# A graph layer on one core: weights' product before the counts, keys' products between the gathers, rows through DRAM, routing in 16 bits

## The chip, the cores and the metric

The kernel runs on one core of one Trainium2 chip. The metric is the device time of one execution in microseconds (us), as the median of several runs. A profile of one execution gives the trace; its span runs from the first to the last instruction, so the execution's own time is a little more. The engines are PE (TensorE, matrix products and transposes), DVE (VectorE), ACT (ScalarE), POOL (GpSimd) and SP (SyncE, which issues most DMAs). Each engine works through its own list of instructions in order.

## What is computed

The input is x, 1250 tokens (nodes of a graph) of 768 numbers, and 41250 edges (src, dst). The layer is, cut to what matters:

```python
xn = layer_norm(x)
out1 = gat_conv(layer_norm(xn) * g + b, ..., H=4, C=192)     # graph attention, 4 heads
out2 = gat_conv(out1, ..., H=2, C=96)                        # graph attention, 2 heads
x = x + concat([xn, out2]) @ Wu + bu + linear_attention(xn)  # q, k = elu + 1; 12 heads
y = layer_norm(x)
gate = y @ Wg + bg; scores, idx = top_k(gate, 2)             # 8 experts
x = x + sum over the two experts: score * (gelu(y @ W1 + b1) @ W2 + b2)

# gat_conv, per head, for each edge s -> d (self loops added):
e = leaky_relu(s_src[s] + s_dst[d], 0.2)
alpha = exp(e - max over d's edges) / sum over d's edges
out[d] = sum of alpha * h[s]
```

## The kernel before

The tokens stand in 10 tiles (NT) of 125 (PT); 768 is 6 chunks (KC) of 128. All products are in float32, where PE makes two passes of each, but for the one-hot products of the counts, which are bfloat16. The code is written for a framework (Tile) that schedules each engine's list itself: the source order is a guide, and work with no dependence on what stands before it in the source can be listed earlier. Semaphores, buffers (a tile's `bufs`) and memory that one pool frees for another set what waits.

*Start, 0 to 21 us.* Edge indices, the weights W1 and W2 and small vectors are loaded from SP's queue; the edges are turned; a branch (`tc.If`, L240) for unsorted edges is not taken.

*Counts and features, 21 to 215 us.* `chunk` counts the edges of 1024 a time: DVE makes two one-hot tiles (`l_hot`, `k_hot`, L335), PE multiplies them (`ec`, L350) and DVE adds the result to the count matrix AT (L356). `features(t)` normalises one tile, PE transposes it (`turn`, L319) and the copy into `xnT` is DVE's (L321). `weights()` folds W1, W2 and the attention vectors into one matrix Wg1 (transposes of W1 L394, products with W2e L405, each W2e product waiting for the reduction L383); it is called after tile 1's features. `gathered(t)` multiplies xnT by Wg1 (L430). Then AT is turned into a mask (L461 to L466).

*Graph attention, 219 to 592 us.* `attend` handles one head. For the first layer's 4 heads: the sources' scores, less their least value, are spread as one row over all partitions (`across`: 10 transposes L504 and three ACT copies L506, into `ss_row`); ten DVE instructions (`scr`, L515) take for each target the maximum over its neighbours; from that come two columns, spread as `up_row` and `dn_row` by `across` again. Then 10 steps `st`, one for each tile of sources: ACT makes two exponentials (L533, L534), DVE takes their maximum (L535) and multiplies by the counts (L536), both 125 x 1250, and PE sums: 10 products a step in layer 1 (`ag`, L548), 3 in layer 2 (L569). Each head's result goes into h2, which the second layer's 2 heads read. `w` has 3 buffers, `v` 2, `ss_row`, `up_row` and `dn_row` one.

*Keys and values.* For each tile, four products of 6 chunks (K and V, two halves each, L607) and two of `kv` (L621), with DVE's `ky` and `ke` (L611 to L614) and sums `kvacc` (L627). They stand behind attention in the source, and the scheduler lists them into attention's gaps.

*Queries and routing, 612 to 920 us.* `graph.close()` frees attention's memory, and Wo, Wq and Wu are loaded there (L588). Per tile: the query (L751), the sum of its products (`po`, L781, `u`, L792), the store, a normalise, the gate, the two best experts, and the place of each token in its expert's list. The places come from `pp` (L830: a triangle times the selection, ones times the running sum) and go, with the gate, by one-hot products into `inv` (L854: `hot` 125 x 128 times `put` 125 x 160), from which `idx` and `gs` are read at the end.

*Experts, 948 us to the end.* Rows of the normalised tokens (`xl_d` in DRAM) are gathered by index, turned (L912), multiplied by the expert's two matrices (L926, L938), scaled by the gate and added to the output by an indirect DMA. A last part handles what does not fit the 3 fixed blocks of an expert.

Of the kernel before, what the change touches and what calls it, by code (L numbers as in the profile page):

```python
# [54 lines left out]
FIX = 3  # L55
# [14 lines left out]
def gps_block(ctx: ExitStack, tc: tile.TileContext, x, src, dst, norm_g, norm_b, W1, a_src1, a_dst1,  # L70
# [60 lines left out]
    xl_d = dram.tile([N + 128, D], F32)  # L131
# [23 lines left out]
    load_tile(0)  # L155
# [4 lines left out]
    nb_row = fl.tile([96, D], F32)  # L160
    nc.sync.dma_start(W1_sb, W1.rearrange("(c p) f -> p c f", p=128))
# [6 lines left out]
    for t, a in zip(a2, (a_src2, a_dst2)):  # L168
        nc.sync.dma_start(t.rearrange("p h c -> p (h c)"), row_bcast(a, 96))
    nc.sync.dma_start(nb_row, row_bcast(norm_b, 96))  # L170

    rows = fl.tile([KC, 128], F32)
    colv = const.tile([128, KC], F32)
    nc.sync.dma_start(rows, norm_g.rearrange("(c p) -> c p", p=128))
    rows96 = fl.tile([26, 96], F32)
    col96 = const.tile([96, 26], F32)
    nc.sync.dma_start(rows96[0:8], b1.rearrange("(c p) -> c p", p=96))
    nc.sync.dma_start(rows96[8:10], b2.rearrange("(c p) -> c p", p=96))
    for k, a in enumerate((a_src1, a_dst1)):
        nc.sync.dma_start(rows96[10 + 8 * k:18 + 8 * k], a.rearrange("h (c p) -> (h c) p", p=96))  # L180
# [145 lines left out]
    with tc.tile_pool(name="ma_p", bufs=2, space=PSUM) as ma_p:  # L326
# [31 lines left out]
        def features(t):  # L358
            if 0 < t < NT - 1:
                load_tile(t + 1)  # L360
            xt = xts.pop(t)
            xn = ln.tile([PT, D], F32, name="xn")
            mv, rs = normalise(xn, xt)

            v2 = small.tile([PT, 1], F32, name="v2")
            nc.vector.tensor_scalar(v2, mv[:, 1:2], rs, rs, op0=ALU.mult, op1=ALU.mult)
            nc.scalar.activation(v2, v2, AF.Sqrt, bias=eps[:PT])
            nc.vector.reciprocal(rs2[:, t:t + 1], v2)
            turn(xnT[:, :, t * PT:(t + 1) * PT], xn, ma_p, "tr", nc.vector.tensor_copy)

        def weights():
# [6 lines left out]
            for k in range(2):  # L378
                pr = fw.tile([96, 2, D], F32, name="W1T", bufs=2).rearrange(
# [58 lines left out]
        with tc.tile_pool(name="hot", bufs=2) as hot, \  # L438
                tc.tile_pool(name="ec_p", bufs=2, space=PSUM) as ec_p:
            for t in range(NT):  # L440
# [3 lines left out]
                if t == 1:  # L444
                    weights()
# [6 lines left out]
                if t == 4:  # L452
# [27 lines left out]
    def least(ss, H):  # L480
# [9 lines left out]
        lo = small.tile([PT, 2, H], F32, name="lo")  # L490
        nc.vector.tensor_copy(lo[:, 0], p[:, 0, :H])
        nc.vector.tensor_scalar(lo[:, 1], p[:, 0, :H], -1.0, None, op0=ALU.mult)
        return lo

    def attend(ss, sd, lo, wp, rb, gather):

        def across(cols, name, bufs, bias=0.0):

            row = rb.tile([PT, N], F32, name=name, bufs=bufs)
            for g0 in range(0, NT, 4):  # L500
                n = min(4, NT - g0)
                p = four()
                for q in range(n):
                    nc.tensor.transpose(p[:, q], cols[:, g0 + q:g0 + q + 1].to_broadcast([PT, PT]),  # L504
                                        ident[:PT, :PT])
                nc.scalar.activation(row[:, g0 * PT:(g0 + n) * PT],  # L506
                                     p[:, :n].rearrange("p a b -> p (a b)"), AF.Identity, bias=bias)
            return row


        ss_row = across(ss, "ss_row", 1, lo[:, 1:2])
        top = small.tile([PT, NT], F32, name="top")
        for t in range(NT):
            scr = wp.tile([PT, N], BF16, name="scr", bufs=1)
            nc.vector.tensor_tensor_reduce(scr, ss_row, mask[:, t], 1.0, 0.0, ALU.mult, ALU.max,  # L515
                                           top[:, t:t + 1])

        nc.vector.scalar_tensor_tensor(top, top, lo[:, 0:1], sd, op0=ALU.add, op1=ALU.add)
        nc.vector.scalar_tensor_tensor(top, top, SLOPE, top, op0=ALU.mult, op1=ALU.max)
        up = small.tile([PT, NT], F32, name="up")  # L520
        dn = small.tile([PT, NT], F32, name="dn")
        sl = small.tile([PT, NT], F32, name="sl")
        nc.vector.tensor_sub(up, sd, top)
        nc.vector.scalar_tensor_tensor(dn, sd, SLOPE, top, op0=ALU.mult, op1=ALU.subtract)
        nc.vector.tensor_scalar(sl, ss, SLOPE, None, op0=ALU.mult)
        up_row = across(up, "up_row", 1)
        dn_row = across(dn, "dn_row", 1)
        for st in range(NT):


            w = wp.tile([PT, N], F32, name="w", bufs=3)
            v = wp.tile([PT, N], F32, name="v", bufs=2)
            nc.scalar.activation(w, up_row, AF.Exp, bias=ss[:, st:st + 1])  # L533
            nc.scalar.activation(v, dn_row, AF.Exp, bias=sl[:, st:st + 1])  # L534
            nc.vector.tensor_tensor(w, v, w, op=ALU.max)  # L535
            nc.vector.scalar_tensor_tensor(w, w, 2.0, AT[:, st, :N], op0=ALU.min, op1=ALU.mult)  # L536
            gather(st, w)

    lo1 = least(s1[:, :, :, 0], H1)
    with tc.tile_pool(name="wp", bufs=3) as wp, tc.tile_pool(name="rb", bufs=1) as rb:  # L540
        with tc.tile_pool(name="ag_p1", bufs=1, space=PSUM) as ag_p:
            for hd in range(H1):
                ag = ag_p.tile([PT, NT // 2, 512], F32, name="ag")

                def gather1(st, w):
# [6 lines left out]
                attend(s1[:, :, hd, 0], s1[:, :, hd, 1], lo1[:, :, hd], wp, rb, gather1)  # L552
                v = ag[:, :, :2 * CG].rearrange("p a (b c) -> p a b c", b=2)
                rd = small.tile([PT, NT // 2, 2, 1], F32, name="rd")
                nc.vector.reciprocal(rd, v[:, :, :, C2:C2 + 1])
                for t in range(NT):
                    nc.vector.scalar_tensor_tensor(h2[:, t], v[:, t // 2, t % 2], rd[:, t // 2, t % 2],
                                                   h2[:, t], op0=ALU.mult, op1=ALU.add)
# [3 lines left out]
        lo2 = least(h2[:, :, at:at + H2], H2)  # L562
        with tc.tile_pool(name="ag_p2", bufs=1, space=PSUM) as ag_p:
            for hd in range(H2):
                ag = ag_p.tile([C2 + 1, 3, 512], F32, name="ag")

                def gather2(st, w):
# [4 lines left out]
                attend(h2[:, :, at + hd], h2[:, :, at + H2 + hd], lo2[:, :, hd], wp, rb, gather2)  # L572
                for i, (a, b) in enumerate(NCH):
                    nc.scalar.copy(o2T[:, hd, a:b], ag[:, i, :b - a])
# [22 lines left out]

    for t in range(NT):
        ky = kp.tile([PT, D], F32, name="ky", bufs=2)
        va = kp.tile([PT, KC, 129], F32, name="va")  # L600
        nc.gpsimd.memset(va[:, :, 128:], 1.0)
        for k in range(2):
            half = slice(k * 384, (k + 1) * 384)
            for w in (Wk_sb, Wv_sb):
                ps = bank()
                for c in range(KC):
                    nc.tensor.matmul(ps[:PT, :384], xnT[:, c, t * PT:(t + 1) * PT], w[:, c, half],  # L607
                                     start=c == 0, stop=c == KC - 1)
                if w is Wk_sb:
                    ke = kp.tile([PT, 384], F32, name="ke", bufs=1)  # L610
                    nc.vector.tensor_add(ky[:, half], ps[:PT, :384], bk_b[:, half])  # L611
                    nc.vector.tensor_scalar(ke, ky[:, half], 0.0, None, op0=ALU.min)
                    nc.scalar.activation(ke, ke, AF.Exp)
                    nc.vector.scalar_tensor_tensor(ky[:, half], ky[:, half], 0.0, ke, op0=ALU.max,  # L614
                                                   op1=ALU.add)
                else:
                    nc.scalar.copy(va[:, 3 * k:3 * k + 3, :128],
                                   ps[:PT, :384].rearrange("p (b c) -> p b c", b=3))
            ps = bank()
            for c in range(3):  # L620
                nc.tensor.matmul(ps[:, c * 129:(c + 1) * 129],  # L621
                                 ky[:, (3 * k + c) * 128:(3 * k + c + 1) * 128], va[:, 3 * k + c],
                                 start=c == 0, stop=c == 2, skip_group_check=True)
            acc = kvacc[:, 3 * k:3 * k + 3]
            got = ps[:, :387].rearrange("p (b c) -> p b c", b=3)
            if t:
                nc.vector.tensor_add(acc, acc, got)  # L627
            else:
                nc.vector.tensor_copy(acc, got)
# [56 lines left out]
    zero = fp.tile([128, D], F32)  # L686
    nc.gpsimd.memset(zero, 0.0)
    nc.sync.dma_start(xl_d[N:], zero)
    nc.sync.dma_start(out[N:], zero)
# [4 lines left out]
    gs = fp.tile([128, NV + 1], F32)  # L694
# [4 lines left out]
    with ExitStack() as rs:  # L699
# [7 lines left out]
        def numbers(shape, pattern, base, mult, name):  # L707
            t = rp.tile(shape, F32, name=name)
            nc.gpsimd.iota(t, pattern=pattern, base=base, channel_multiplier=mult,
                           allow_small_or_imprecise_dtypes=True)  # L710
            return t
# [304 lines left out]
```

## Time and profile before

| | |
|---|---|
| median of 5 runs | 1178.35 us (1176.38 to 1179.51) |
| profiled execution | 1179.27 us |
| its span | 1177.3 us, mean granted clock 0.971 |
| PE busy, weight loads | 1077.2 us (91%), 723.4 us (61%) |
| DVE, ACT, POOL busy | 668.8 (57%), 358.1 (30%), 76.4 us (6%) |
| moved by DMA | 79.62 MB, mean 68 GB/s |

In the page's slices, each digit is the busy share of one fortieth of the span in tenths. A group's line gives busy time, mean duration of one instruction in ns, and the idle time of the engine just ahead of it with what ended it. A timeline's line gives start, length, engine, line, operation and, in brackets, the idle time before it and its releaser. The largest groups are the first layer's gathers (L548, 137.4 us of PE), the expert products (L926 and L938, 100.6 each), and on DVE the three 125 x 1250 instructions of attention (L515, L535, L536, 86 to 87 us each).

### The profile page before, as it was taken

Reading aid. Unit: us, or ns where it says so; the run is one execution under the profiler, and the core shown is the slowest. Engines: PE = TensorE matmul, PEld = TensorE weight load, DVE = VectorE, ACT = ScalarE, POOL = GpSimd, SP = SyncE. Lnnn points to the kernel's source line nnn. Section 1 sums busy time; section 2 is a strip of 40 time slices with the busy share of each in tenths; the row PEclk is TensorE's granted clock in tenths of the full one; section 3 lists DMA queues with packets and bytes.
Section 4 is the critical chain, followed back from the end, with each engine's and each line's share of the span. In section 5 each row is a group of like instructions: output and inputs, shape, how many; then the busy total and the mean of one; then the engine's idle time right before and its main releaser. Section 6 shows DMA issues by size and latency. Waiting matters only on the chain.

```text
span 1177.3 us, 12106 instructions
## 1 busy us (share of the span) xinstructions
PE 1077.2 (91%) x4583; PEld 723.4 (61%) x4583; DVE 668.8 (57%) x1366; ACT 358.1 (30%) x527; POOL 76.4 (6%) x100
## 2 busy tenths in 40 slices
PE   2699988999999999988989999999999589999993
PEld 2586656578888778544545666666666356666652
DVE  7866676669696966696922555555555422222211
ACT  2231114373737373373712211111111011111111
POOL 1000000000000000000000000000000122322321
PEclk9999998999999999989989999999999789999997
DMA  5014000000000001000083111111123527777533
GB/s 156 27 66 148 25 16 1 1 1 1 1 1 1 1 1 53 1 0 1 1 323 99 40 40 40 40 40 40 39 65 106 189 93 188 201 211 217 122 56 55
DMA packets 33283, 79.62 MB, mean 68 GB/s; under 512 B 5259, under 2 KB 13021, under 8 KB 33209
## 3 DMA queue, kind: packets, MB, share of 16 engines
q1 hardware_dynamic: 27608, 59.02, 15.3%
q0 software_dynamic: 5600, 19.66, 8.1%
q8 instruction: 40, 0.66, 0.2%
q14 instruction: 35, 0.28, 0.1%
HBM read 60.37 MB, written 18.30 MB: 67 GB/s over the span
## 4 chain that ended last, share of the span: by engine, by line
PE 70%; DVE 20%; DMA 3%; issue 2%; ACT 2%; POOL 0%; DVEq 0%; SPq 0%; POOLq 0%; ACTq 0%
PE po L781 13%; PE ph L926 8%; PE py L938 7%; PE mm L430 7%; PE mm L607 7%; PE mm L751 7%; DVE scr L515 6%; DVE w L535 5%; DVE w L536 5%; PE ag L548 3%; PE ag L569 2%; PE u L792 2%; PE px L912 2%; PE mm L405 2%; DMA w<-in_L_gnn_Wu_dram 2%
## 5 line engine op out<-in xcount | busy, mean ns | idle before, releaser
L548 PE MATMUL ag<-kept,w 125*125 125x198 f32 x800 | 137.4, 333 | 5.1 <-DVE w L536 4.9
L548 PEld LDWEIGHTS ag<-kept,w 125*125 125x125 f32 x800 | 133.5, 188 | 9.0 <-DVE w L536 9.0
L926 PE MATMUL ph<-xsT,w 128*128 128x384 f32 (+1 forms) x324 | 100.6, 470 | 1.7 <-DVE xsT L915 1.7
L938 PE MATMUL py<-w,hT 128*128 128x384 f32 x300 | 100.6, 486 | 0.0
L430 PE MATMUL mm<-Wg,xnT 128*125 128x400 f32 x240 | 91.7, 520 | 1.0 <-DVE xnT L321 0.6
L607 PE MATMUL mm<-Wv_sb,xnT 128*125 128x384 f32 x240 | 85.7, 489 | 4.8 <-DVE kvacc L627 4.8
L535 DVE TENSOR_TENSOR w<-v,w 125x1250 f32<-125x1250 f32 x60 | 86.3, 1453 | 6.6 <-ACT w L533 5.9
L781 PE MATMUL po<-w,xnT 128*125 128x384 f32 x240 | 84.8, 496 | 2.9 <-DMA w<-in_L_gnn_Wu_dram 2.9
L515 DVE CUSTOM_DVE_ANT_0 scr<-ss_row,mask 125x1250 bf16<-125x1250 f32 x60 | 87.2, 1453 | 0.5 <-ACT ss_row L506 0.2
L536 DVE SCALAR_TENSOR_TENSOR w<-w,AT 125x1250 f32<-125x1250 f32 x60 | 86.4, 1454 | 0.4
L926 PEld LDWEIGHTS ph<-xsT,w 128*128 128x128 f32 x324 | 59.7, 193 | 41.3 <-DVE xsT L915 2.3
L607 PE MATMUL mm<-Wk_sb,xnT 128*125 128x384 f32 x240 | 84.4, 486 | 0.0
L534 ACT ACTIVATE v<-dn_row,sl 125x1250 f32<-125x1250 f32 x60 | 79.3, 1333 | 16.9 <-DVE w L535 16.4
L751 PE MATMUL mm<-w,xnT 128*125 128x384 f32 x240 | 84.2, 489 | 0.0
L915 DVE COPY xsT<-px 128x384 f32<-128x384 f32 x50 | 25.5, 552 | 100.5 <-PE px L912 100.5
L781 PE MATMUL po<-w,qT 128*125 128x384 f32 x240 | 80.8, 486 | 0.0
L938 PEld LDWEIGHTS py<-w,hT 128*128 128x128 f32 x300 | 55.3, 190 | 33.9
L941 DVE TENSOR_TENSOR ys<-py,wb 128x768 f32<-128x768 f32 x25 | 23.9, 957 | 72.5 <-PE py L938 48.8
L781 PEld LDWEIGHTS po<-w,xnT 128*125 128x125 f32 x240 | 44.2, 190 | 30.5 <-DMA w<-in_L_gnn_Wu_dram 3.1
L781 PEld LDWEIGHTS po<-w,qT 128*125 128x125 f32 x240 | 44.2, 188 | 29.4
L607 PEld LDWEIGHTS mm<-Wv_sb,xnT 128*125 128x125 f32 x240 | 42.4, 187 | 31.1 <-DVE kvacc L627 6.9
L751 PEld LDWEIGHTS mm<-w,xnT 128*125 128x125 f32 x240 | 43.6, 188 | 27.6 <-ACT qT L321 0.2
(274 smaller groups left out, 1414.5 us busy)
## 6 DMA issues: line engine op xcount, KB each, us to landing
w<-in_L_ffn_W_dram SPq DMA_DIRECT2D x18, 1152.0 KB
xt<-in_x_dram SPq DMA_DIRECT2D x20, 336.0 KB
wb<-in_L_ffn_b_dram SPq DMA_DIRECT2D x9, 384.0 KB
out_dram<-xt SPq DMA_DIRECT2D x10, 336.0 KB
xl_d<-xl SPq DMA_DIRECT2D x10, 336.0 KB
W_sb<-in_L_gnn_W_dram SPq DMA_DIRECT2D x1, 2304.0 KB
Wk_sb<-in_L_mix_Wk_dram SPq DMA_DIRECT2D x1, 2304.0 KB
Wv_sb<-in_L_mix_Wv_dram SPq DMA_DIRECT2D x1, 2304.0 KB
```

The costliest lines, as they stand in the source:

```text
L430: nc.tensor.matmul(ps[:PT, :2 * (CG + 2)], xnT[:, c, t * PT:(t + 1) * PT], Wg1[:, c, 2 * k:2 * k + 2].rearrange("p h c -> p (h c)"), start ...
L515: nc.vector.tensor_tensor_reduce(scr, ss_row, mask[:, t], 1.0, 0.0, ALU.mult, ALU.max, top[:, t:t + 1])
L534: nc.scalar.activation(v, dn_row, AF.Exp, bias=sl[:, st:st + 1])
L535: nc.vector.tensor_tensor(w, v, w, op=ALU.max)
L536: nc.vector.scalar_tensor_tensor(w, w, 2.0, AT[:, st, :N], op0=ALU.min, op1=ALU.mult)
L548: nc.tensor.matmul(ag[:, t // 2, o:o + CG], w[:, t * PT:(t + 1) * PT], gw[:, st, hd], start=st == 0 and t % 2 == 0, stop=st == NT - 1, ski ...
L607: nc.tensor.matmul(ps[:PT, :384], xnT[:, c, t * PT:(t + 1) * PT], w[:, c, half], start=c == 0, stop=c == KC - 1)
L751: nc.tensor.matmul(ps[:PT, :384], xnT[:, c, tk], Wq_sb[:, c, half], start=c == 0, stop=c == KC - 1)
L781: nc.tensor.matmul(po[k][:, :384], l, r[:, k * 384:(k + 1) * 384], start=i == 0, stop=i == len(parts) - 1)
L915: nc.vector.tensor_copy(xT[:, 3 * a:3 * a + 3, j * 128:(j + 1) * 128], px[:, a, :384].rearrange("p (b n) -> p b n", b=3))
L926: nc.tensor.matmul(ph[:, :n * 128], w[0][:, o:o + 128], xT[:, c, :n * 128], start=c == 0, stop=c == KC - 1)
L938: nc.tensor.matmul(py[:, k, :384], hT[:, f, j * 128:(j + 1) * 128], w[:, o:o + 384], start=f == 0, stop=f == FC - 1)
```

## The change

1. `weights()` is called before the counts' loop. Eight small loads go from SP's queue to ACT's; the first tile of x is loaded behind W1 and W2; Wk, Wv and bk are loaded at tile 2 instead of 4.
2. The copies of turned tiles into xnT are ACT's.
3. `attend` becomes `layer`, which handles all heads. Only the first head's rows are made by `across`; the other heads' `ss_row` and their two rows (now one tile `row`, 2 buffers) are turned to rows by one transposition (`to_rows`), written to DRAM and loaded with a broadcast. The next head's maxima are written into the first five steps of the head before it, two a step. `v` has one buffer.
4. The keys' products become a generator, `keys_and_values`, of 60 pieces; attention's steps draw one each (in layer 2 three of four), and the rest is drawn after attention.
5. In routing the one-hot tiles, the triangle, ones, the selection and its running sum are float16. `inv` holds the token's number alone. The gate is stored behind the token's row in `xl_d` (776 instead of 768 columns, two small DMAs a tile) and comes back with the gathered row; one DVE copy per gathered block takes it out.

```diff
-    xl_d = dram.tile([N + 128, D], F32)
+    row_d = [dram.tile([n * NT, PT], F32, name=f"row{i}") for i, n in enumerate((H1, H2, 2))]
+    xl_d = dram.tile([N + 128, D + NE], F32)
...
-            turn(xnT[:, :, t * PT:(t + 1) * PT], xn, ma_p, "tr", nc.vector.tensor_copy)
+            turn(xnT[:, :, t * PT:(t + 1) * PT], xn, ma_p, "tr", nc.scalar.copy)
...
+            weights()
             for t in range(NT):
...
-                if t == 1:
-                    weights()
+                if t == 0:
                     setup.close()
...
-                if t == 4:
+                if t == 2:
                     nc.sync.dma_start(Wk_sb, Wk.rearrange("(c p) f -> p c f", p=128))
...
+    def to_rows(cols, d):
+        n = cols.shape[1]
+        p = four()
+        nc.tensor.transpose(p[:n, 0], cols, ident[:PT, :PT])
+        r = small.tile([H1 * NT, PT], F32, name="r", bufs=2)
+        nc.scalar.copy(r[:n], p[:n, 0])
+        nc.sync.dma_start(d, r[:n])
...
+    def layer(ss, sd, H, d, wp, rb, head):
+        lo = least(ss, H)
+        over = small.tile([PT, H, NT], F32, name="over", bufs=1)
+        for h in range(H):
+            nc.vector.tensor_scalar(over[:, h], ss[:, :, h], lo[:, h:h + 1], None, op0=ALU.subtract)
+        to_rows(over.rearrange("p h t -> p (h t)"), d)
+        def scores(h):
+            ss_row = rb.tile([PT, N], F32, name="ss_row")
+            if h:
+                nc.sync.dma_start(ss_row, row_bcast(d[h * NT:(h + 1) * NT], PT))
+            else:
+                across(over[:, h], ss_row)
+            return ss_row
+        def sides_of(h):
+            top = small.tile([PT, NT], F32, name="top")
+            for t in range(NT):
+                scr = wp.tile([PT, N], BF16, name="scr", bufs=1)
+                nc.vector.tensor_tensor_reduce(scr, rows_of[h], mask[:, t], 1.0, 0.0, ALU.mult, ALU.max,
+                                               top[:, t:t + 1])
+                if t % 2:
+                    yield
+            if h + 1 < H:
+                rows_of[h + 1] = scores(h + 1)
...
+            row = rb.tile([PT, 2, N], F32, name="row", bufs=2)
+            if h:
+                to_rows(sides.rearrange("p a t -> p (a t)"), row_d[2])
+                nc.sync.dma_start(row.rearrange("p a n -> p (a n)"), row_bcast(row_d[2], PT))
+            else:
+                for a in range(2):
+                    across(sides[:, a], row[:, a])
...
+                w = wp.tile([PT, N], F32, name="w", bufs=3)
+                v = wp.tile([PT, N], F32, name="v", bufs=1)
...
+                gather(st, w)
+                next(ahead, None)
+                if H == H1 or st % 4 != 3:
+                    next(keys, None)
...
-            xl = rl.tile([PT, D], F32, name="xl")
-            normalise(xl, xt)
+            xl = rl.tile([PT, D + NE], F32, name="xl")
+            normalise(xl[:, :D], xt)
...
-            gate = rl.tile([PT, NE], F32, name="gate")
+            gate = xl[:, D:]
             nc.vector.tensor_add(gate, pg[:PT, :NE], bg_b)
+            for p, tt in token_rows(t):
+                nc.sync.dma_start(xlr[p, tt, D:], gate[p])
...
-                hot = rl.tile([PT, 128], F32, name="hot")
+                hot = rl.tile([PT, 128], F16, name="hot")
...
-                put = rl.tile([PT, 2, NV], F32, name="put")
-                for i, v in enumerate((node1[:, t:t + 1], both[:, 1, k:k + 1])):
-                    nc.vector.tensor_scalar(put[:, i], slot_row, s_f[:, 0, k:k + 1], v,
-                                            op0=ALU.is_equal, op1=ALU.mult)
-                nc.tensor.matmul(inv.rearrange("p a s -> p (a s)"), hot,
-                                 put.rearrange("p a s -> p (a s)"), start=k == 0 and t == 0,
+                put = rl.tile([PT, NV], F16, name="put")
+                nc.vector.tensor_scalar(put, slot_row, s_f[:, 0, k:k + 1], node1[:, t:t + 1],
+                                        op0=ALU.is_equal, op1=ALU.mult)
+                nc.tensor.matmul(inv, hot, put, start=k == 0 and t == 0,
                                  stop=k == 1 and t == NT - 1)
...
+            at = slice(D + e, D + e + 1) if isinstance(e, int) else bass.ds(e + D, 1)
+            nc.vector.tensor_copy(gates[:, j:j + 1], xg[:, at])
```

## The prediction

> **What bounds the kernel now.** I read the page first: the engines' totals, the 40 slices and the chain that ended last.
>
> ```profile
> PE 1077.2 (91%) x4583; PEld 723.4 (61%) x4583; DVE 668.8 (57%) x1366; ACT 358.1 (30%) x527; POOL 76.4 (6%) x100
> ...
> PE   2699988999999999988989999999999589999993
> ...
> PEclk9999998999999999989989999999999789999997
> ...
> PE 70%; DVE 20%; DMA 3%; issue 2%; ACT 2%; POOL 0%; DVEq 0%; SPq 0%; POOLq 0%; ACTq 0%
> ```
>
> TensorE (PE) is busy for 1077.2 of 1177.3 us, so 100 us are idle, and no stage is without it. VectorE (DVE) is 20% of the chain, all of it in the counts and in attention. Next, windows by stage, to see where PE really sets the pace.
>
> ```profile
> 260.00:280.00 20.00, 18.92 (x110) 18.00 (x109) 20.00 (x20) 13.63 (x11) 0.00 (x0) 1.00 0.00 1
> 500.00:505.00 5.00, 3.09 (x15) 1.70 (x13) 3.59 (x4) 5.00 (x8) 0.00 (x0) 1.00 0.00 0
> 505.00:510.00 5.00, 3.78 (x6) 1.74 (x7) 4.97 (x4) 2.11 (x3) 0.00 (x0) 0.51 0.00 0
> 510.00:515.00 5.00, 5.00 (x13) 2.16 (x12) 3.25 (x4) 4.06 (x4) 0.00 (x0) 0.81 0.00 0
> 612.00:920.00 308.00, 307.64 (x1128) 187.63 (x1129) 153.82 (x412) 55.01 (x89) 0.43 (x4) 0.99 0.20 65
> 920.00:950.00 30.00, 14.56 (x54) 10.51 (x53) 13.46 (x60) 1.14 (x3) 5.91 (x6) 0.58 0.52 168
> ```
>
> Columns: window, length, busy time of PE, weight loads, DVE, ACT, POOL, then PE's clock, DMA share and GB/s. From 612 to 920 (queries and routing) PE has no gap: work taken from it there is time. From 920 to 950 it waits for a chain through DVE. At 260 to 280 (attention) DVE is full and PE nearly so; the two trade places within a head. The third view is the timelines where attention hands over:
>
> ```profile
> 253.64 1.45 DVE L535 TENSOR_TENSOR w<-v,w 125x1250 f32<-125x1250 f32 x1
> 255.01 1.45 DVE L515 CUSTOM_DVE_ANT_0 scr<-ss_row,mask 125x1250 bf16<-125x1250 f32 x1
> 256.39 1.45 DVE L536 SCALAR_TENSOR_TENSOR w<-w,AT 125x1250 f32<-125x1250 f32 x1
> ```
>
> ```profile
> 592.40 0.39 SPq L588 DMA_DIRECT2D w<-in_L_mix_Wo_dram  x1
> ...
> 593.42 2.22 SPq L588 DMA_DIRECT2D w<-in_L_gnn_Wu_dram  x1
> ```
>
> ```profile
> 612.28 2.92 PE L781 MATMUL po<-w,xnT 128*125 128x384 f32 x4 [2.94 <-DMA w<-in_L_gnn_Wu_dram]
> ```
>
> The next head's maxima (scr) already stand between this head's two products, so a step takes DVE 3 x 1.375 = 4.12 us (the starts are 1.375 apart). And PE enters the routing stage when Wu lands, 612.28 - 592.40 = 19.9 us after attention frees the memory, with the last keys' products used up at 609. So what attention must give is an earlier end of attention, not less PE work.
>
> **The change, part by part.** The order in which each engine lists its instructions is known for both kernels; durations come from this one execution (1179.27 us, span 1177.3, thus 1.97 outside; it is 0.92 above the median of 1178.35). The rows I price with:
>
> ```profile
> L504 PE MATMUL rb<-ident,up 125*125 125x125 f32 x60 | 9.7, 276 | 0.1
> L504 PE MATMUL rb<-ident,dn 125*125 125x125 f32 x60 | 9.7, 275 | 0.0
> ...
> L854 PE MATMUL inv<-put,hot 125*128 125x160 f32 x40 | 9.1, 347 | 1.9 <-DVE put L852 1.9
> L830 PE MATMUL g<-cum,ones 125*128 125x8 f32 x20 | 3.9, 266 | 0.0
> L830 PE MATMUL g<-sel,tri 125*128 125x8 f32 x20 | 3.3, 240 | 1.9 <-DVE sel L826 1.9
> ...
> L350 PE MATMUL ec<-k_hot,l_hot 128*125 128x120 bf16 x324 | 29.9, 239 | 11.4 <-DVE AT L356 8.5 <-DVE k_hot L335 2.9
> ```
>
> *Weights ahead, copies to ScalarE.* PE has little but counts at 20 to 60 us. `weights()` now starts there, but its W2e products need DVE's two multiplies and two reductions (1.72 and 1.74 us each), so PE stands some 7 us first and DVE's counts begin about 10 us later. DVE gets 10.5 us back from the 20 xnT copies, so the last counts still end at about 189, as now. Behind them the new order has 5 gathered products instead of 12 (7 x 0.72, from 198.35 to 199.07 on PE's timeline, = 5.0 us less), the last tile's transposes no longer wait (2.8 less), and four V products more (4 x 0.645, six in 3.87, = 2.6 more): attention's first scr comes 5.2 earlier, **-5** (from -7 to 0, the latter if the late counts are not caught up). The eight small loads moved from SP to ACT's queue issue ahead of ACT's edge copies: 0 to +1, taken as 0 because ACT is idle from 3 to 7.8 us.
>
> *Rows through DRAM.* The 180 transposes of L504 (PE 29.0 us with the 60 of ss and h) become 66: 114 x 0.161 = 18.4 us of PE work less. That is worth its full price only if PE stays supplied. For every head but the first, the row now comes by a broadcast DMA; there is none such in the trace, but the 125-partition bias rows at 448 to 461 us are the same shape of transfer:
>
> ```profile
> DMA  0003413333332331323333332333333320789833
> GB/s 0 0 0 123 104 66 123 132 132 132 123 132 104 57 57 76 142 113 132 132 142 123 123 132 113 123 142 132 123 123 142 142 104 0 183 312 180 236 123 123
> ```
>
> They use three tenths of the DMA engines at about 130 GB/s (the 128-partition bv behind them reaches 312), and start 0.9 us after issue. A head's ss_row (625 KB) is thus 0.9 + 4.8 + about 1.0 to release = 6.7 us; its up and down row (1.25 MB) 0.9 + 9.6 + 1.0 = 11.5, behind a small write that I take at 2.3 (bounds 0.9, the start alone, and 4).
>
> *First head.* DVE's list has head 1's first scr directly behind head 0's last, and it waits for ss_row. Five scr stand ahead of the first w. So: scr(0) 16.5 us (219.3 to 235.8 now), wait 6.7, five scr and two key evacuations 7.8, then max, scr, min 4.2: 35.2 us to the first ag against 252.4 - 219.3 = 33.1 now; with the semaphores **+3** (0 to 6).
>
> *Keys between the gathers.* The generator gives one key step per gather, but the scheduler ran some 15 steps ahead before the first gather. PE's list therefore has 60, then 90 ag with no key product between. Those 15 steps go at DVE's 4.12 us (PE needs 3.4): 61.8. Head 1's row is not in time: transposition 3.5 after step 5, copy 1, write 2.3, load 11.5, exps 2.7 = 21 against 17.5 us of DVE cover, 4 us of stall (0 to 8). The last 25 steps are PE's: 25 x 3.4 + 9 x 0.7 (kv) + 16 x 3.87 (K and V) = 153. Together 219 us against 461.1 - 252.4 = 208.7: **+10** (0 to +18). In heads 2 and 3 a step takes 6.1 us and both trips hide.
>
> *Between the layers.* As for the first head, layer 2's first w now sits behind a wait of 6.7 and six scr instead of the `across` chain: 44.8 us become 50.6, **+6** (+1 to +9).
>
> *Layer 2.* v has one buffer, so an exp waits for the max before it: 1.33 + 1.45 and two hand-overs, about 3.0 us a step, 20 steps 60; head 1's row trip has 12 us of cover, 7 us of stall; 6 to the end. That is 73 us where 506.2 to 592.4 were 86: **-13** (-20 to -4); the gap between the heads has gone.
>
> *The clock.* In 500 to 505 PE waits 1.39 and 1.74 us, and the next two windows are granted 0.51 and 0.81: 0.49 x 3.78 + 0.19 x 5.00 = 2.8 us lost. I add one more such restart after head 1's stall, **+3** (0 to +6). [...]
>
> Sum for attention: -5 + 3 + 10 + 6 - 13 + 3 = **+4**. Wu, and PE with it, come 4 us later, about 616; the keys' products that now cover until 609 end near 606, so the 114 transposes saved come back as PE waiting.
>
> *16-bit routing.* inv: 40 passes of 160 columns become 20 of 80; at ec's 29.9/324 = 0.092 us, 1.8 instead of 9.1. The pp pair: 20 instead of 40 passes at 0.092 to 0.17, 1.8 to 3.4 instead of 7.2. Nine tenths of these 11 to 13 us lie inside 612 to 920: **-10** (-6 to -12). In the end gap the tenth tile's chain loses two `put` (0.23 apart), the gs copy and most of 1.56 us of inv at the lower clock: **-2** (-3 to 0). The gate's 20 small writes lie behind xl's on SP; the next x tile's load is queued behind them, but is not needed for one tile (31 us): 0. The 25 gate copies on DVE (0.15 each beside 43 us of DVE work in 200) and the 776-wide rows: 0 (0 to +2).
>
> Total: +4 - 10 - 2 = -8; span 1169.3, execution 1171.3, on the median's footing 1170.
>
> **The rivals.** *PE stays supplied* (1147): the trips are shorter, or other work fills in, and attention ends as much earlier as PE's work shrank, 18; with 12 from routing 1177 - 30. For it: PE's work from 21 us to the last kv falls from 534 to 516. Against it: 15 gathers without a key product between, and the DVE step of 4.12.
>
> *The trips decide* (1187; slower). Six fixed parts lie open on the path: two ss_row waits, and two row trips with a write and a read each. I have 1.9 to 2.3 us for one. If it is 2.1 more (4 us), the six cost 12.6 and the two ss_row waits that 7.8 us of DVE work just cover cost 4 more: +16.6, with -8 about +9. It decides from 1.4 us more per part (8/6). For it: DVE waits with w and the key evacuations queued behind, and those free PE's banks; no write and read back of a row is in this trace. Against it: the 0.9 us start.
>
> *Nothing is left* (1178): the first 15 steps and layer 2 run some 8 us slower than said and eat routing's gain. The spread maxima bring nothing in any case: the timeline has them spread already.
>
> **How the numbers follow.** The likeliest sum 0.46 (its own range 1162 to 1175), PE supplied 0.18, nothing left 0.08, trips 0.28. Faster by over 0.2% is the first two, 0.64; within 0.2% (2.4 us, about what a measurement of this kernel can tell) 0.08; slower 0.28. From 1146 to 1190 leaves out about half of the second and the upper third of the last case.
>
> **What would show it.** Right: ss_row loads of 6 to 7.5 us at 130 GB/s; PE's idle between 250 and 320 grown to 15 us or more; Wo's issue at 590 to 600; inv under 2.5 us in all; the stretch from Wu's landing to the last u product 10 us shorter. Wrong: Wo issued before 580 (PE supplied) or after 605 (trips), inv and pp together above 8 us, or a new wait in 612 to 920.

## The result, and the profile after

| | before | changed |
|---|---|---|
| median | 1178.18 us (71 runs, 1172.29 to 1181.67) | 1181.38 us (41 runs, 1175.83 to 1184.76) |
| profiled execution, its span | 1179.27, 1177.3 us | 1176.44, 1174.3 us |
| two more profiled executions | | 1182.51 and 1182.99; 1180.5 and 1180.9 us |

The ratio of the times is 1.002, 95% interval 1.0012 to 1.0028: slower by 3.2 us by the medians and by 2.4 by the ratio, where 8 us faster was forecast. The page of the changed kernel, with the rows that answer to those shown of before:

```profile
PE 1051.7 (90%) x4428; PEld 701.0 (60%) x4428; DVE 660.4 (56%) x1343; ACT 352.6 (30%) x517; POOL 76.7 (7%) x99
...
PE   2899889977789999978888999999999589999994
...
PEclk9999999989799999989998999999999789999998
...
PE 75%; DVE 9%; DMA 8%; issue 2%; ACT 2%; POOL 0%; SPq 0%; DVEq 0%; POOLq 0%; ACTq 0%
```

PE has 25.5 us less to do and the span is 3 us shorter, so idle time took most of it. DVE's share of the chain fell from 20% to 9%, and DMA has 8%, half of it the broadcast rows (`row<-row`, 4%). This execution is 4.9 us under the median of its kernel, while that of before is 1.1 over its own. The second execution is as far above its median (1.1) as that of before, so those two are compared stage by stage. Times in us, from the starts in the timelines; po stands for the products `po<-w,xnT`, the first half of each tile's sum; "forecast" is before plus the prediction's term.

| stage | before | forecast | changed, first | changed, second |
|---|---|---|---|---|
| to the first scr | 219.3 | 214.3 | 214.0 | 218.1 |
| first scr to first ag | 33.1 | 36.1 | 35.4 | 35.7 |
| layer 1, first to last ag | 208.7 | 218.7, clock +3 | 227.6 | 228.0 |
| to layer 2's first ag | 45.1 | 51.1 | 52.7 | 51.1 |
| layer 2, to Wo's issue | 86.2 | 73.2 | 71.3 | 72.9 |
| Wo's issue to first po | 19.9 | 19.9 | 20.6 | 20.7 |
| first to last po | 296.0 | 286 | 289.6 | 289.9 |
| last po to the end | 269.0 | 267 | 263.1 | 264.1 |

Layer 1 stands out. The waits of PE from the first scr on (engine, line, releaser; us in total, times, longest), first execution:

```profile
PE ag L631 <- DVE h L640: 10.2, 1, 10.2
PE ag L631 <- DVE w L577: 9.2, 6, 6.5
PE po L840 <- DMA w<-in_L_gnn_Wu_dram: 8.3, 1, 8.3
PE mm L611 <- DVE ky L603: 7.8, 3, 5.5
```

Before, the largest row of this view was 4.9 us in ten waits. The first line is the hand-over from head 0 to head 1. The timelines there, first of ACT, then of DVE, then of PE; the row's read was issued at 276.48:

```profile
288.50 1.34 ACT L574 ACTIVATE w<-row,s 125x1250 f32<-125x1250 f32 x1 [7.74 <-DMA row<-row]
```

```profile
291.09 1.46 DVE L576 TENSOR_TENSOR w<-v,w 125x1250 f32<-125x1250 f32 x1 [4.83 <-ACT v L575]
292.47 1.45 DVE L537 CUSTOM_DVE_ANT_0 scr<-ss_row,mask 125x1250 bf16<-125x1250 f32 x1
...
293.85 1.46 DVE L577 SCALAR_TENSOR_TENSOR w<-w,AT 125x1250 f32<-125x1250 f32 x1
295.22 0.21 DVE L638 RECIPROCAL rd<-ag 125x10 f32<-125x10 f32 x1
295.35 1.40 DVE L576 TENSOR_TENSOR w<-v,w 125x1250 f32<-125x1250 f32 x1
296.67 3.40 DVE L640 SCALAR_TENSOR_TENSOR h<-ag,rd,h 125x198 f32<-125x198 f32 x10
```

```profile
286.32 3.62 PE L631 MATMUL ag<-kept,w 125*125 125x198 f32 x20 [0.50 <-DVE w L577]
300.12 12.21 PE L631 MATMUL ag<-kept,w 125*125 125x198 f32 x54 [10.19 <-DVE h L640]
```

The row comes 12.0 us after its read is issued and DVE waits 4.83 us for the exponentials, both as forecast. But head 0's result still lies in PE's banks: the reciprocal (`rd`) and the ten `h` that take it out are listed on DVE behind head 1's first maximum, which waits, and `h` behind its second too. Head 1's first `w` is ready at 295.3 (293.85 + 1.46); PE starts at 300.12, when the `h` are done. Then the clock (length, busy time of PE, weight loads, DVE, ACT, POOL, granted clock, DMA share, GB/s):

```profile
290.00:295.00 5.00, 0.00 (x0) 0.00 (x0) 3.91 (x4) 4.70 (x4) 0.00 (x0) 0.74 0.00 0
295.00:300.00 5.00, 0.00 (x0) 0.00 (x0) 5.00 (x14) 1.49 (x2) 0.00 (x0) 0.50 0.00 0
300.00:305.00 5.00, 4.88 (x15) 4.88 (x16) 5.00 (x6) 1.34 (x1) 0.00 (x0) 0.50 0.00 0
305.00:310.00 5.00, 5.00 (x29) 5.00 (x28) 4.36 (x6) 1.80 (x2) 0.00 (x0) 0.90 0.00 0
```

PE does nothing from 290 to 300, and its next 5 us go at half the clock, 0.50 x 4.88 + 0.10 x 5.00 = 2.9 us lost. Last, the issue of Wo, where attention frees its memory, and the first product behind it:

```profile
601.02 0.40 SPq L679 DMA_DIRECT2D w<-in_L_mix_Wo_dram  x1
```

```profile
621.58 2.89 PE L840 MATMUL po<-w,xnT 128*125 128x384 f32 x4 [8.35 <-DMA w<-in_L_gnn_Wu_dram]
```

The wait of 2.94 us for Wu has become 8.35 though the first product comes only 0.7 us later behind Wo's issue (20.6 for 19.9): there is less work left to cover the load. From PE's list, the key work still undone at Wo's issue is worth 6.5 us (0.645 for a K or V product, 0.245 for a kv) for 11.1 before.

### The profile page after: what moved, and what is told of

Its sections match the earlier page's. It is cut to its first block, busy times and chain, and to the rows that moved or that the text cites. A ratio compares the mean times of both kernels' runs of the same rounds, so it can differ in the third digit from the quotient of the medians.

```text
span 1174.3 us, 11831 instructions
## 1 busy us (share of the span) xinstructions
PE 1051.7 (90%) x4428; PEld 701.0 (60%) x4428; DVE 660.4 (56%) x1343; ACT 352.6 (30%) x517; POOL 76.7 (7%) x99
## 4 chain that ended last, share of the span: by engine, by line
PE 75%; DVE 9%; DMA 8%; issue 2%; ACT 2%; POOL 0%; SPq 0%; DVEq 0%; POOLq 0%; ACTq 0%
PE po L840 14%; PE ph L985 8%; PE ag L631 8%; PE py L997 8%; PE mm L595 7%; PE mm L431 7%; PE mm L810 7%; DMA row<-row 4%; DVE scr L537 3%; PE u L851 2%; PE ag L656 2%; DVE w L576 2%; PE ec L351 2%; DMA w<-in_L_gnn_Wu_dram 2%; PE mm L406 2%
## 5 line engine op out<-in xcount | busy, mean ns | idle before, releaser
L631 PE MATMUL ag<-kept,w 125*125 125x198 f32 x800 | 145.4, 341 | 19.4 <-DVE h L640 10.2
L631 PEld LDWEIGHTS ag<-kept,w 125*125 125x125 f32 x800 | 139.6, 194 | 26.5 <-DVE w L577 11.5
L575 ACT ACTIVATE v<-row,sl 125x1250 f32<-125x1250 f32 x60 | 80.2, 1337 | 76.0 <-DVE w L576 63.0
L537 DVE CUSTOM_DVE_ANT_0 scr<-ss_row,mask 125x1250 bf16<-125x1250 f32 x60 | 87.2, 1454 | 11.5 <-DMA ss_row<-row 9.2
L431 PE MATMUL mm<-Wg,xnT 128*125 128x400 f32 x240 | 87.8, 508 | 0.2 <-ACT xnT L322 0.2
L972 DVE COPY xsT<-px 128x384 f32<-128x384 f32 x50 | 25.5, 552 | 87.4 <-PE px L969 87.4
L574 ACT ACTIVATE w<-row,s 125x1250 f32<-125x1250 f32 x40 | 53.4, 1335 | 42.2 <-PE ag L631 34.3
L840 PEld LDWEIGHTS po<-w,xnT 128*125 128x125 f32 x240 | 43.3, 190 | 36.6 <-issue 10.9
L840 PEld LDWEIGHTS po<-w,qT 128*125 128x125 f32 x240 | 44.1, 188 | 29.5 <-issue 0.2
```

The lines of the kernel that those rows point to most:

```text
L431: nc.tensor.matmul(ps[:PT, :2 * (CG + 2)], xnT[:, c, t * PT:(t + 1) * PT], Wg1[:, c, 2 * k:2 * k + 2].rearrange("p h c -> p (h c)"), start ...
L537: nc.vector.tensor_tensor_reduce(scr, rows_of[h], mask[:, t], 1.0, 0.0, ALU.mult, ALU.max, top[:, t:t + 1])
L574: nc.scalar.activation(w, row[:, 0], AF.Exp, bias=ss[:, st, h:h + 1])
L575: nc.scalar.activation(v, row[:, 1], AF.Exp, bias=sl[:, st:st + 1])
L631: nc.tensor.matmul(ag[:, t // 2, o:o + CG], w[:, t * PT:(t + 1) * PT], gw[:, st, hd], start=st == 0 and t % 2 == 0, stop=st == NT - 1, ski ...
L840: nc.tensor.matmul(po[k][:, :384], l, r[:, k * 384:(k + 1) * 384], start=i == 0, stop=i == len(parts) - 1)
```

## The experiments

My theory after the traces: the loss is the order in which DVE and PE list their work at the hand-over of heads, with the keys' products not standing where PE waits. The rivals: the trips through DRAM are simply too long; attention is bound by DVE whatever the order; or the loss is at the end, where Wu is no longer covered.

For most runs one account of PE is enough: the stretch from the first scr to Wo's issue, what PE does and does not do in it, and what key work is left. All from windows of the profiled execution of each.

| kernel | stretch | PE busy | PE idle | clock | key work left | wait ahead of the first po |
|---|---|---|---|---|---|---|
| before | 373.1 | 350.7 | 22.4 | 0.99 | 11.1 | 2.9 |
| changed (second) | 387.7 | 344.4 | 43.3 | 0.96 | 6.5 | 8.4 |
| 115 + 10 | 375.7 | 341.0 | 34.7 | 0.97 | 10.5 | 6.9 |
| finish first | 376.7 | 343.4 | 33.2 | 0.97 | 6.5 | 10.8 |
| 112 + 13 | 367.8 | 337.9 | 29.9 | 0.98 | 10.5 | 6.9 |
| 112 + 13, 36 draws | 358.6 | 329.1 | 29.5 | 0.98 | 19.0 | 0 |
| 36 draws | 383.9 | 336.5 | 47.4 | 0.96 | 15.0 | 0 |

The profiled executions lie from 3.4 us under the median of their kernel (112 + 13, 36 draws) to 4.6 over it (112 + 13), so a difference of a few us between two rows is not safe by itself.

**Routing alone.** The kernel before with part 5 only (float16 one-hots, gate stored with the row).

```diff
-    xl_d = dram.tile([N + 128, D], F32)
+    xl_d = dram.tile([N + 128, D + NE], F32)
-                hot = rl.tile([PT, 128], F32, name="hot")
+                hot = rl.tile([PT, 128], F16, name="hot")
```

> The kernel before with the 16-bit routing alone (part 5). Theory (routing is on PE's path, attention took its gain back): PE loses about 9 us of inv and pp and the end gap 2 to 3 us, so 8 to 12 us less than before, a ratio of 0.990 to 0.993. Rival (routing's PE work is replaced by another wait, the small gate writes or the clock): less than 3 us, ratio above 0.997.

Ratio to before 0.9919 (0.9897 to 0.994), 1168.60 us: 9.6 less. Attention is untouched (373.1 us from the first scr to Wo's issue in both kernels). So parts 1 to 4 cost 1181.4 - 1168.6 = 12.8 us.

**Early weights and routing, old attention.** Before with parts 1, 2 and 5.

```diff
-                if t == 1:
-                    weights()
+            weights()
+            for t in range(NT):
-            turn(xnT[:, :, t * PT:(t + 1) * PT], xn, ma_p, "tr", nc.vector.tensor_copy)
+            turn(xnT[:, :, t * PT:(t + 1) * PT], xn, ma_p, "tr", nc.scalar.copy)
```

> The kernel before with parts 1, 2 and 5 (weights' product ahead, ACT copies, 16-bit routing), attention and keys as before. Theory: the 5 us that the first scr came earlier carry through an unchanged attention, 13 to 17 us less than before, ratio 0.986 to 0.989, and it beats the changed kernel by over 1%. Rival (an earlier start of attention is lost in PE's gaps, since the keys run out earlier): the same as the routing alone within 2 us.

1.0131 (1.011 to 1.0152), 1193.26 us, which neither theory had. The scheduler listed more of the keys' products inside attention: none are left at its end, and Wo is issued at 614.98, 21 us later than in the run before. The first product behind it shows the price:

```profile
636.34 2.89 PE L780 MATMUL po<-w,xnT 128*125 128x384 f32 x4 [19.44 <-DMA w<-in_L_gnn_Wu_dram]
```

From the first scr to Wo's issue PE is busy 13.5 us more than in the run before and idle 14 us more. So the place of the keys' products seems to matter in both kernels; what the work that covers Wu is worth is measured below, with 36 draws.

**Late weights, new attention.** The changed kernel without parts 1 and 2.

```diff
-            weights()
-                if t == 0:
+                if t == 1:
+                    weights()
-            turn(xnT[:, :, t * PT:(t + 1) * PT], xn, ma_p, "tr", nc.scalar.copy)
+            turn(xnT[:, :, t * PT:(t + 1) * PT], xn, ma_p, "tr", nc.vector.tensor_copy)
```

> The changed kernel with parts 1 and 2 undone (weights' product after tile 1, loads as before, xnT copied by DVE); attention's order of keys is the same as in the changed kernel. Theory (attention starts some 6 us later and the rest follows): 5 to 7 us more than the changed kernel, ratio to before 1.006 to 1.009. Rival (the early weights cost time in any kernel, as with the old attention): the same or less than the changed kernel, ratio below 1.001.

1.0081 (1.0057 to 1.0105), 1190.02 us: 8.6 above the changed kernel by the medians, 7 by the ratios. Early weights are worth that here, and the new attention (parts 3 and 4) costs 1190.0 - 1168.6 = 21 us beside the old one.

**No key drawn in attention.**

```diff
-                if H == H1 or st % 4 != 3:
-                    next(keys, None)
```

> The changed kernel without drawing the keys' pieces in attention's steps: all 60 stand behind attention in the source, as before, and the scheduler moves them up. Theory (the scheduler fills PE's gaps either way): within 4 us of the changed kernel, ratio to before 0.998 to 1.006. Rival (the one-per-step order starves the head boundaries, where the old one held keys back): 6 us or more less than the changed kernel, ratio below 0.997.

1.0204 (1.018 to 1.0229), 1200.95 us, slower than either expectation had it. The scheduler did not fill in by itself: 71.1 us of key work stand behind attention, and PE waits at all three hand-overs:

```profile
PE ag L629 <- DVE h L638: 28.4, 3, 10.7
```

No draw of part 4 is in this run, so a hand-over without a key product in it costs about 10 us of PE each. The changed kernel has covered two of them; the first it has not, since its list goes 15 steps without a key product.

**Loads in two pieces, 112 + 13 partitions.** Both broadcast loads of a row (`ss_row` and `row`) are cut so.

```diff
-                nc.sync.dma_start(row.rearrange("p a n -> p (a n)"), row_bcast(row_d[2], PT))
+                for p, n in ((slice(0, 112), 112), (slice(112, PT), 13)):
+                    nc.sync.dma_start(row[p].rearrange("p a n -> p (a n)"), row_bcast(row_d[2], n))
```

> The changed kernel with each broadcast load of ss_row and row split into 112 and 13 partitions, nothing else. [...] Rival (the hand-overs wait for the finish of the last head and for DVE's pace, trips are covered): under 3 us less, ratio 0.999 to 1.003.

0.9844 (0.9819 to 0.987), 1160.38 us: 21 less than the changed kernel, where I had expected 10 to 16 if the trips set the hand-overs. The trip from the read's issue (278.90) to the exponential is 7.6 us for 12.0:

```profile
286.47 1.34 ACT L576 ACTIVATE w<-row,s 125x1250 f32<-125x1250 f32 x1 [4.21 <-DMA row<-row]
```

But two things changed: with two DMAs in place of one, the scheduler also moved the first key step (6 kv and 12 K passes) from five steps into head 1 to the hand-over, and three scr in front of head 1's first maximum. The run with 115 + 10, below, takes these apart.

**Finish first.** The first maximum of heads 1 to 3 of layer 1 is made to depend on the head before it being taken out of PE's banks (it is multiplied by one, made from `h2`).

```diff
+                if h and st == 0 and H == H1:
+                    nc.vector.tensor_scalar(one, h2[:, NT - 1, 0:1], 0.0, 1.0, op0=ALU.mult, op1=ALU.add)
+                    nc.vector.scalar_tensor_tensor(w, v, one, w, op0=ALU.mult, op1=ALU.max)
```

> The changed kernel with one thing made to depend on another: in layer 1, the first max of heads 2 to 4 is multiplied by a one that is read from h2, so that DVE lists the finish of the head before (reciprocal and ten sums from PSUM) ahead of it. The scheduler then also lists some key products between heads 1 and 2. Theory (PE's 10.2 us at that hand-over are the finish, which stands behind the first w of the next head while that waits for its row): 5 to 10 us less than the changed kernel, ratio to before 0.994 to 0.998. Rival (the row's trip alone sets the hand-over): within 2 us of the changed kernel, ratio 1.000 to 1.004.

0.9935 (0.9917 to 0.9952), 1171.77 us, 10 less. That agrees with the theory's number, but not with its reason. PE at the hand-over:

```profile
290.60 0.83 PE L616 MATMUL mm<-va,ky 125*128 125x129 f32 x6
291.26 4.04 PE L600 MATMUL mm<-Wk_sb,xnT 128*125 128x384 f32 x12
298.60 4.49 PE L600 MATMUL mm<-Wv_sb,xnT 128*125 128x384 f32 x8 [3.30 <-DVE kvacc L622]
302.93 13.56 PE L636 MATMUL ag<-kept,w 125*125 125x198 f32 x80
```

Head 1's gathers do not start sooner: 302.9 - 251.0 = 51.9 us after the first gather of all, for 50.7 and 50.0 in two executions of the changed kernel. What differs is 0.8 + 4.0 + 4.5 = 9.4 us of keys' products done while they are waited for (the last at less than full clock, 0.85 from 295 to 300 and 0.80 from 300 to 305). Layer 1 takes 215.8 us for 228.0, with the same 68.5 us of key work in it by PE's list. The list had moved these products too, and five maxima in front of head 1's first `w`, so the run doesn't show what listing the finish first is worth alone.

**Loads in two pieces, 115 + 10 partitions.** The same edit with other numbers. PE's list is that of 112 + 13, instruction for instruction.

```diff
-                for p, n in ((slice(0, 112), 112), (slice(112, PT), 13)):
+                for p, n in ((slice(0, 115), 115), (slice(115, PT), 10)):
```

> The changed kernel with both row loads cut 115 + 10 partitions instead of 112 + 13. TensorE's list is the one of e3_split to the instruction (its first key step, 4.6 us, stands at the hand-over from head 0 to head 1), but the larger piece keeps the narrow pattern of the whole load, so the trip should stay near the changed kernel's. So e3_split against this run is the price of the trips alone, and this run against the changed kernel that of the key step's place alone. Trips theory (e3_split's 21 us are the shorter trips): row read to first exp 11 us or more, 2 to 6 us under the changed kernel, 1175 to 1179, ratio to before 0.998 to 1.001; attention ends at 597 to 600. Place theory (the key step at the hand-over keeps TensorE's clock up, and that is most of it): 1162 to 1168, ratio 0.987 to 0.991, with the row read still 11 us.

0.9911 (0.9882 to 0.994), 1168.49 us. The load moves at 0.29 of the DMA engines, as the whole row did, the trip is as long as ever, 291.28 - 278.70 = 12.6 us, and still 13 of the 21 us are there: the lists have most of it, and the trips the other 8, since the lists of both runs are the same. PE at the hand-over:

```profile
291.07 0.83 PE L613 MATMUL mm<-va,ky 125*128 125x129 f32 x6
291.75 4.03 PE L597 MATMUL mm<-Wk_sb,xnT 128*125 128x384 f32 x12
300.08 11.97 PE L633 MATMUL ag<-kept,w 125*125 125x198 f32 x60 [4.30 <-DVE w L579]
```

Head 1's gathers start 49.0 us after the first one, 1 to 2 us sooner than in the changed kernel, behind 4.7 us of keys' products. Layer 1 takes 218.5 us for 228.0, close to what was forecast, and PE does the same 68.5 us of key work in it in both. These 9.5 us, and not all 13, are what the hand-over can be given: by the profiles, the way to the first ag (34.3 for 35.7) and the one between the layers (48.8 for 51.0) are shorter too, where DVE now lists one maximum less ahead of the first `w`. That 4 us more of key work are left at the end won nothing that shows: layer 2 to Wo's issue takes 74.1 us for 73.0, and the first po comes 22.4 us behind Wo's issue for 20.7.

**36 draws for 40.** No key step is drawn at st 9 of layer 1, the loads as they are.

```diff
-                if H == H1 or st % 4 != 3:
+                if (H == H1 and st != 9) or (H == H2 and st % 4 != 3):
```

> The changed kernel with no key step drawn at st 9 of layer 1 (36 draws for 40), loads as they are: key work left at the end of attention 15.0 us by TensorE's list, against 6.5. Theory of the uncovered Wu: the 8.3 us that TensorE waits for Wu shrink by what is left over and attention ends up to 8 us sooner, so 6 to 9 us under the changed kernel: 1172 to 1175, ratio 0.995 to 0.998. Rival (TensorE waits in attention for the row trips and the key steps taken out come back as waiting there): attention ends as in the changed kernel at about 601, Wu's wait goes to 0 but the left-over products come behind: 1180 to 1184, ratio 1.001 to 1.005.

0.9965 (0.9944 to 0.9986), 1174.49 us: 6.9 less than the changed kernel, as the theory of the uncovered Wu had it. PE waits for Wu no more. In the profiled execution, which is 3.5 us above the median of its kernel, attention is 3.8 us shorter, not 8.5 as the key work left over (15.0 for 6.5) would make it, since 4.1 us of it came back as idle time (the table).

**Both: 112 + 13 and 36 draws.** The edits shown above, together.

> The changed kernel with the broadcast loads split into 112 and 13 partitions, and with no key piece drawn at the last step of each head of layer 1 (36 instead of 40). By PE's list 19 instead of 10.5 us of key products are then left at the end of attention. Theory (they cover the 20 us in which Wo, Wq and Wu are loaded): 5 to 8 us less than the split alone, ratio to before 0.977 to 0.980. Rival (what is not drawn is missing inside attention): the same as the split alone, ratio 0.983 to 0.987.

0.9805 (0.9788 to 0.9822), 1156.63 us: the fastest here, 22 us under before (1178.77 on the same chip), but 3.8 under the split alone where 5 to 8 were expected. PE's account, for the changed kernel's first execution and for this one:

```profile
214.00:601.02 387.02, 344.88 (x1503) 255.12 (x1502) 302.93 (x391) 180.41 (x178) 2.68 (x9) 0.96 0.07 24
```

```profile
215.40:573.96 358.56, 329.08 (x1457) 243.52 (x1456) 297.89 (x380) 179.32 (x175) 2.58 (x8) 0.98 0.09 26
```

That attention is bound by DVE whatever the order does not hold: DVE is busy for 302.9 and 297.9 us in these two, 5 us less, and the stretch is 28 us shorter.

**These two and finish first.**

> All three: split loads, finish first, 36 pieces. Theory: with short trips the finish is nearly covered, so 0 to 4 us less than without it, ratio to before 0.974 to 0.980, the fastest so far. Rival (the multiplied max or the shifted keys cost as much): 1 to 3 us more than without it.

0.987 (0.9854 to 0.9885), 1162.65 us: 6 us worse than without it, which neither expectation had. With short trips the row is there, and a first maximum held until the finish only delays head 1: its gathers start 52.8 us after the first of all, for 48.1 without it. Finishing first is no cure by itself.

**Two more profiles of the changed kernel.**

> The changed kernel once more, for a second profiled execution. If the spread of its runs is the granted clock behind attention's waits, the mean clock is 0.955 to 0.962, the span 1177 to 1183, and the 1 to 8 us over the first profile lie between 290 and 330, 500 and 530 and 600 and 630 us, none between 630 and 920. If it lies elsewhere (HBM, the end gap), those stretches are as in the first profile to 1 us.

> As look1_after, a third profiled execution: clock theory, its span and its mean clock stand in one order with those of the other two (0.965 at 1174.3), and the stretches that differ are those behind a wait of TensorE.

Spans 1180.5 and 1180.9 us at clocks of 0.959 and 0.957, for 1174.3 at 0.965. Span and clock stand in one order, as expected, but the place was missed: 4.2 and 4.4 of the 6.2 and 6.6 us are there before the first scr, in the counts. One wait there on PE's timeline, in the first execution and then in the second:

```profile
157.11 0.54 PE L320 MATMUL tr<-ident,xn 125*128 125x125 f32 x3 [2.31 <-DVE xn L312]
```

```profile
158.27 0.89 PE L320 MATMUL tr<-ident,xn 125*128 125x125 f32 x3 [2.31 <-DVE xn L312]
```

The same wait of 2.31 us stands ahead of the same three passes; they take 0.54 us behind it in one execution and 0.89 in the other, where the clock granted from 160 to 165 is 0.87 for 1.00, and from 190 to 195, behind a wait of 2.24 us, 0.79 for 1.00. Layer 1 and layer 2 agree within 2 us in all three, so the loss in attention is no matter of the draw.

## Why the prediction was wrong

**The step that failed is the term "keys between the gathers", +10 (0 to +18)**, with the clock's +3 beside it: layer 1 took 19.3 us more, not 13. Of its parts, the pace (15 steps at 4.12 us), the row's trip (11.5 forecast, 12.0) and DVE's stall (4 forecast, 4.83) were right. What was wrong was to carry DVE's stall over to PE as it stood. In the second execution head 1's first step starts 303.82 - 289.90 = 13.9 us after head 0's last in place of 4.1, so 9.8 were lost, not 4: 4.95 are DVE's stall there, and 4.8 pass between the first `w` (299.0) and PE's start, while DVE ends the finish of head 0. I had read that 90 products stand in PE's list with no key product between them, and that the first w waits; I had not looked where the finish of the head before, which frees PE's banks, stands in DVE's list: behind that same wait. Two runs show what it was worth to have key work there: finish first, where head 1 starts no sooner, brought layer 1 from 228.0 to 215.8 us, and 115 + 10, with trips no shorter and head 1 hardly earlier, to 218.5, against 218.7 forecast, both with the same key work in the layer. So the 9.8 us cost what they did because PE's list held nothing to do in them. That the finish stood behind the wait is read from the list; putting it ahead, with maxima moved as well, did not shorten the gap.

**Stage A, -5.** Right in size but a noisy term: the first execution gives -5.3, the other two -1.2 and -0.9. Over the eleven profiles shown or used here with early weights the first scr comes at 214.0 to 218.4 (mean 216.1), over the three with late ones at 219.3 to 221.6 (220.6): -4.5. Against the execution that matches the median this is 3.8 of the 11 us missed; by these means it was mostly the draw that differed, not the mechanism.

**First head +3, gap +6, layer 2 -13.** Measured +2.3 and +2.6; +7.6 and +6.0; -14.9 and -13.3. The trip of `ss_row` took 6.2 us (231.03 to 237.24) for 6.7, the row's write 1.27 for 2.3 (at the next head 2.2 to 2.4, in the three executions).

**Wu.** It was said that the saved transposes come back as PE waiting for Wu; they do, 8.4 us. But I took Wu at 616 and attention 4 us longer; Wo is issued at 601.0 and 605.8 (592.4 before), which is the miss of layer 1 carried on. The sign by which I would have named the rival of the trips (after 605) is at the border, and yet the trips were a little shorter than priced; that rival has the right side by the wrong mechanism. Its price per part was not the cause: 115 + 10 gains 13 us with the same trips. Still, 8 us are to be had from them.

**Routing -10, end -2.** Alone -9.6 in all. `inv` was priced at 1.8 us by the bfloat16 row and costs 4.1; `pp` costs 3.4, the upper bound:

```profile
L913 PE MATMUL inv<-put,hot 125*128 125x80 f16 x20 | 4.1, 204 | 1.8 <-DVE put L911 1.7
...
L891 PE MATMUL g<-sel,tri 125*128 125x8 f16 x10 | 1.7, 170 | 1.9 <-DVE sel L887 1.9
L891 PE MATMUL g<-cum,ones 125*128 125x8 f16 x10 | 1.7, 167 | 0.0
```

The 20 products of 80 columns take 204 ns each and 4.1 us in all, so none of them overlaps the next; the row I took for them, 239 ns for 120 columns with 29.9/324 = 0.092 us a piece, was of products that overlap. The first to last po stretch is 6.1 us shorter, and the rest lies behind the last po.

Against the matching execution the misses add up: stage A 3.8, layer 1 with its clock 6.3, routing and end 1.0, the rest 0.1, together 11.2, which is -8 turned into +3.2. What stays open: how the 9.5 us of layer 1 divide between the key product and the three scr that moved with it, which no run had apart; PE's timelines speak for the product (4.7 us of work in the wait, and the clock at 0.66 and then 1.00 from 300 to 310, for 0.50 and 0.69 in the second execution, whose gathers start at 303.8).

## What to carry to other kernels

When a load is put between two stages, follow the stall on every engine: look in each list at what stands behind the waiting instruction, above all what frees the next stage's buffers, and price the gap on the engine that sets the pace, not on the one that waits first. Independent work is a budget to be placed: here its best places were a hand-over (with 4.7 us of it there, layer 1 gave back 9.5) and the end, under a load that nothing else covers. And where a few us decide, take several profiles: this kernel's executions differed by 6 us of span, 4 of them in a stage that was not in question.

## What was not expected of the hardware

*The broadcast over 125 partitions was slow, in 112 + 13 less so.* From 0.7 to 0.9 us after its issue to its use, the whole row moved at 0.29 of the DMA engines and 111 GB/s; cut in 112 + 13, at 0.68 and 184; cut in 115 + 10, at 0.29 and 107. Why the cut at 112 moves so much wider than the one at 115, no run shows.

*The clock after a wait.* Behind 10.2 us without work PE had 0.50 from 300 to 305 and 0.90 from 305 to 310, and was back at 1.00 from 310 on, 10 us after its restart at the most. Behind waits of 2.2 to 2.3 us in the counts it had 1.00 in one execution, 0.79 to 0.87 in another, so the length of such a wait alone did not tell what it cost.

*The row's way through DRAM was short.* The read of `row` was issued 1.27 us after its write (275.21 to 276.48), and 2.2 to 2.4 us at the next head; the dear part is the broadcast behind it, 12.0 us to its use.
